# A bidirectional Mamba-2 mixer on one core: square sums between the halves of the output projection, D x ahead of x times the step sizes, and decays and step sizes at other places

## The chip, the cores and the metric

The kernel runs on one core of one Trainium2 chip. A core has a matrix engine (TensorE, PE in the profile; PEld is the loading of its weights), a vector engine (VectorE, DVE), an activation engine (ScalarE, ACT), a general engine (GpSimd, POOL), and an engine that here only starts transfers (SyncE, SP). Each engine has its own queue and takes its instructions in that order; between engines they wait for one another's results. SBUF is the memory on the chip, PSUM the one that TensorE writes to.

The metric is the time of one launch on the device in microseconds. Before the change its median is 1506.12 us over three runs (1503.04 to 1506.87). The profiled execution spans 1499.7 us. All data are fp32.

## What is computed

The input is an image batch of 8 x 32 x 32 x 128, that is 8 sequences of 1024 tokens with 128 channels. Three residual parts follow one another: attention, the mixer, and a spectral filter. Only the mixer concerns us. For each sequence it runs twice, forward (`d = 0`) and backward in time (`d = 1`), with two sets of weights, and adds both to the residual:

```python
def _mamba3(x, in_proj, conv_w, conv_b, A_log, dt_bias, D, norm_w, out_proj):   # x: layer-normed tokens
    z, xbc, dt = split(x @ in_proj)
    xbc = silu(conv(xbc, 4 taps) + conv_b)
    xh, Bm, Cm = split(xbc)                       # 4 heads of 64; state of 64
    dt = softplus(dt + dt_bias);  A = -exp(A_log)
    y = _ssd(xh, dt, A, Bm, Cm) + xh * D          # "D x"
    yg = y * silu(z)
    yn = yg * rsqrt(mean(yg * yg, -1) + EPS) * norm_w     # "square sums"
    return yn @ out_proj

def _ssd(xh, dt, A, Bm, Cm):                      # chunks of 64 tokens
    xdt = xh * dt[..., None];  dA = dt * A        # "x times step sizes", decays
    Acs = cumsum(dA within a chunk)
    Y_diag = (C B^T * exp(segment sums of dA)) @ xdt
    states = B^T @ (exp(Acs_last - Acs) * xdt)    # one for each chunk
    prev   = scan over chunks: state = states + state * exp(Acs_last)
    Y_off  = exp(Acs) * C @ prev
    return Y_diag + Y_off

h = _mamba3(x, fwd...) + _mamba3(x[:, ::-1], bwd...)[:, ::-1]
t = t + h
```

## The kernel before

The mixer works through 16 units, one for each sequence and direction: (b, 0), (b, 1), for b from 0 to 7. In a unit, x and its gates lie channel by token as two tiles of 128 x 1024 (`n = 0, 1`); what goes into the states lies token by channel. The units are interleaved by hand three deep: one pass of the loop at L1169 does the middle of unit `u`, the beginning of unit `following`, and the end of unit `last`. The loop stands under a manual schedule in which each engine takes its instructions in the order in which the program issues them. So the order of the calls in the loop is the order of each queue, and a call that stands earlier is not only earlier itself: what stands behind it on the same engine waits with it.

In the order of one pass, with the lines that later steps name:

- `turn_decays` and `take_decays` of `following` (L807, L813): the cumulated decays, turned by TensorE, their exponentials on ScalarE, and a trip through memory (`cd`) that brings them back as rows for all partitions in `lm` and `ec`. `between(u, Exp)` (L852, L855) is ScalarE's exponential over `lm`, two pieces of 128 x 1024.
- `turn_x` (L940): 16 transposes of x into two PSUM buffers (`sx`, L948), each followed by VectorE's multiplication with the step sizes, `xdt` (L951). `weigh_start` (L859) multiplies `ec` with C on GpSimd. `add_x(last)` (L1068) is D x of the unit before, added to its outputs in PSUM (`y`, L1074).
- `turn_b` (L958): B and C B^T into one PSUM buffer (`sb`), copied by ScalarE (`bg`, L973). In a forward unit, `turn_tokens` then turns the next sequence's tokens (`px`, copied to `xt`).
- `project_x(following, n)` (L877): `pp`, its copy to `xp` on ScalarE (L886); `first_tap` (L889, L891) begins the convolution over 4 tokens on ScalarE. `gate(last, n)` (L1083): VectorE's product with silu(z) (L1085) and ScalarE's square (L1086). `decayed_x`: `xdd` (L982).
- In a forward unit, the first part of `steps` (L476) for the next sequence: `pd` (L491) on TensorE, `sp_v` (L499), L501 and L502 on VectorE, an exponential on ScalarE (L503), L505 on VectorE. The parts behind its two `yield`s, the logarithm (L508) and L510 to L515, come after `add_up`.
- `project_out(last)` (L1088): `spo`, 16 calls that the trace counts as 32 matmuls (L1092). `square_sums` (L1100): eight matmuls with a matrix of ones into `misc` (L1104), copied by ScalarE to `sums` (L1112). `turn_sums` (L1114): two transposes back into `misc` (L1118), `rms_v` on VectorE (L1120) and the power -1/2 on GpSimd, `rms` (L1122). `add_up` (L1126, L1129): the residual takes `spo` times `rms`.
- The three taps of the convolution on VectorE (`convolve`, L895, L899): those of half 0 lie between the square sums and the add-up, those of half 1 near the end of the pass. `project_z` (L906): `pz` and its silu (L910). `activate_x` (L903, L904): silu of the convolved x.
- `normalize` and `normalized` (L442, L451): in a backward unit, the layer norm of the sequence after the next: `bn_stats`, a power on GpSimd, the shift (L453), and eight pieces of `ln_x` on ScalarE (L458).
- `from_row` (L842, L846): GpSimd forms `lm` = cs - row for `following`. It is made to wait for the last tap that was issued ("beside the states"), so that it runs beside the state steps.
- `chunk_states` (L986): `pst`, two PSUM buffers. `pass_states` (L1003): 28 short steps on VectorE (L1012). `weigh_decays` (L1030, L1034), `between(following, Relu)`, `project_bc` and `activate_bc` (L912 to L935) of `following`: `pb` on TensorE and four silus.
- `outputs(u, 0)` and `outputs(u, 1)` (L1038): `sy`, the matmuls at L1060, with `add_decays` (L792: `pdec` on TensorE, two copies on ScalarE) of the unit after the next between them.

PSUM is the scarce memory: `ps_w` and `ps_s` are two pools of two buffers each, every buffer 128 x 1024. `sx`, `sb`, `px`, `pp`, `pd`, `pz`, `pb` and `pdec` take turns in `ps_w`; `spo`, `misc`, `pst` and `sy` in `ps_s`. A buffer is written again only when its last reader is done.

Of the kernel before, what the change touches and what calls it, by code (L numbers as in the profile page):

```python
# [9 lines left out]
AF = mybir.ActivationFunctionType  # L10
# [4 lines left out]
P = 128  # L15
B = 8
T = 1024
NT = T // P
# [27 lines left out]
def fast_kernel(ctx: ExitStack, tc: tile.TileContext, a: dict, out: bass.AP, bad: bass.AP):  # L46
# [713 lines left out]
    with ExitStack() as s:  # L760
# [104 lines left out]
        def projected(u, cols, name):  # L865
            ps = wide_psum(ps_w, name)
            for i in range(2):
                nc.tensor.matmul(
                    ps[:, i * 512 : (i + 1) * 512],
                    lhsT=win[u.d][:, cols],  # L870
                    rhs=u.seq["xt"][:, pad + i * 512 : pad + (i + 1) * 512],
                    start=True,
                    stop=True,
                )
            return ps

        def project_x(u, n):  # L877

            if n == 0:
                u.xs = p2.tile([P, 2, T], F32, tag="xs", name=f"xs{u.tag}")  # L880
                u.xp = []
            pp = projected(u, slice(DI + n * P, DI + (n + 1) * P), f"pp{u.tag}_{n}")
            xp = p2.tile([P, T + pad], F32, tag="xp", name=f"xp{u.tag}_{n}")
            body, edge = (slice(pad, T + pad), slice(0, pad)) if u.d == 0 else (slice(0, T), slice(T, T + pad))
            nc.gpsimd.memset(xp[:, edge], 0.0)
            nc.scalar.copy(xp[:, body], pp)  # L886
            u.xp.append((xp, body))
# [18 lines left out]
        def project_z(u, n):  # L906
            if n == 0:
                u.zs = p2.tile([P, 2, T], F32, tag="zs", name=f"zs{u.tag}")
            pz = projected(u, slice(n * P, (n + 1) * P), f"pz{u.tag}_{n}")
            nc.scalar.activation(u.zs[:, n, :], pz, AF.Silu)  # L910

# [175 lines left out]

        def project_out(u):  # L1088
            u.po = wide_psum(ps_s, f"spo{u.tag}").rearrange("p (j e) -> p j e", j=NT)
            for j in range(NT):  # L1090
                for n in range(2):
                    nc.tensor.matmul(  # L1092
                        u.po[:, j, :],
                        lhsT=u.y[:, n, j * P : (j + 1) * P],
                        rhs=wo[u.d][:, n, :],
                        start=(n == 0),
                        stop=(n == 1),
                    )
# [48 lines left out]
        s.enter_context(tc.manual_schedule(engines=ALL_IN_ORDER))  # L1147
        first, norms, av = units[0], {}, avs[1]
        add_decays(first)
        turn_decays(first)  # L1150
# [3 lines left out]
        for n in range(2):  # L1154
            project_x(first, n)
            first_tap(first, n)
        convolve(first, 0)
# [7 lines left out]
        compare_denominators(most, least, wide_psum(ps_w, "pf")[0:1, :2])  # L1165
        add_decays(units[1])

        last = None
        for at, u in enumerate(units):  # L1169
            following = units[at + 1] if at + 1 < len(units) else None  # L1170

            fresh = u.b + 1 if u.d == 0 and u.b + 1 < B else 0
            if following:
                turn_decays(following)
            if at == 0:
                between(u, AF.Relu, 1.0)
            if following:
                take_decays(following)
            between(u, AF.Exp, -1.0)
            turn_x(u)  # L1180
            weigh_start(u, u.convolved)
            if last:
                add_x(last)
            turn_b(u)
            if fresh:
                turn_tokens(fresh, seqs[fresh], wide_psum(ps_w, f"px{fresh}"))
            if following:
                project_x(following, 0)
                first_tap(following, 0)
            if last:  # L1190
# [3 lines left out]
            if last:  # L1194
                gate(last, 1)
            decayed_x(u)
            going = iter(())
            if fresh:
                going = steps(fresh, seqs[fresh], wide_psum(ps_w, f"pd{fresh}"))
                next(going)  # L1200
                next(going)
            if last:
                project_out(last)
                misc = wide_psum(ps_s, f"misc{last.tag}")
                square_sums(last, misc)
            if following:
                first_tap(following, 1)
                convolve(following, 0, range(pad - 1))
            if last:
                turn_sums(last, misc)  # L1210
            if following:
                convolve(following, 0, range(pad - 1, pad))
            project_z(u, 0)
            project_z(u, 1)
            if following:
                activate_x(following, 0)
# [8 lines left out]
            pass_states(u)  # L1225
            if norm:
                for _ in normalized(b, bridge, *norm):
                    pass
            if last and last.d == 1:
# [8 lines left out]
            outputs(u, 0)  # L1238
            if at + 2 < len(units):
                add_decays(units[at + 2])  # L1240
            if following:
                activate_x(following, 1)
            outputs(u, 1)
            last = u
        add_x(last)
        for n in range(2):
            gate(last, n)
        project_out(last)
        misc = wide_psum(ps_s, f"misc{last.tag}")
        square_sums(last, misc)  # L1250
        turn_sums(last, misc)
        add_up(last)
# [1068 lines left out]
```

## Time and profile before

| Stage (us of the span) | PE | DVE | ACT | POOL | clock |
|---|---|---|---|---|---|
| attention, 0 to 456 | 431.62 | 360.53 | 293.52 | 235.17 | 0.98 |
| mixer, 456 to 1086 | 544.79 | 495.30 | 397.16 | 186.31 | 0.96 |
| transform, 1086 to 1176 | 85.09 | 45.05 | 43.11 | 61.30 | 0.97 |
| frequencies, 1176 to 1450 | 266.33 | 201.16 | 149.56 | 32.96 | 0.99 |
| inverse, output, 1450 to 1500 | 30.98 | 21.17 | 0.00 | 0.00 | 0.84 |

The columns are busy microseconds of each engine in the stage, from the table by windows; the last is the mean clock that TensorE was granted, as a share of full speed. A stage of 630 us in which TensorE is busy for 545 and VectorE for 495 has a good deal of idle time on every engine. In the page's list of groups the costliest of the mixer are these (mean duration of one, and how many):

| Group | mean ns | count |
|---|---|---|
| L859 `ec` on POOL, 128x2048 | 4532 | 16 |
| L899 tap on DVE, 128x1024 | 1282 | 96 |
| L919 `pb` on PE, 128x512 | 598 | 256 |
| L1012 state step on DVE, 128x64 | 275 | 448 |
| L951 `xdt` on DVE, 128x1024 | 1221 | 32 |
| L1122 `rms` on POOL, 128x8 | 2455 | 16 |

A line of an engine's order of time gives the start in the span, the time to the end of the group, the engine, the line, the operation, out<-in with shape, the count, and in brackets how long the engine was idle before it and whose result ended that.

### The profile page before, as it was taken

Reading aid. Unit: us, or ns where it says so; the run is one execution under the profiler, and the core shown is the slowest. Engines: PE = TensorE matmul, PEld = TensorE weight load, DVE = VectorE, ACT = ScalarE, POOL = GpSimd, SP = SyncE. Lnnn points to the kernel's source line nnn. Section 1 sums busy time; section 2 is a strip of 40 time slices with the busy share of each in tenths; the row PEclk is TensorE's granted clock in tenths of the full one; section 3 lists DMA queues with packets and bytes.
Section 4 is the critical chain, followed back from the end, with each engine's and each line's share of the span. In section 5 each row is a group of like instructions: output and inputs, shape, how many; then the busy total and the mean of one; then the engine's idle time right before and its main releaser. Section 6 shows DMA issues by size and latency. Waiting matters only on the chain.

```text
span 1499.7 us, 45232 instructions
## 1 busy us (share of the span) xinstructions
PE 1358.8 (91%) x19782; PEld 855.7 (57%) x19782; DVE 1123.2 (75%) x2250; ACT 883.4 (59%) x1293; POOL 515.7 (34%) x510
## 2 busy tenths in 40 slices
PE   5999999999998989888988898897589899999977
PEld 2333323333334656565655666665479898999962
DVE  5788888788766788888888787886655577777744
ACT  2766666676676666666676667664155455555520
POOL 2336866776202232323232323233177211111100
PEclk9999999999999899999999999999799999999989
DMA  7001111110003333343334343341158522232258
GB/s 184 28 1 29 54 33 43 50 43 8 1 1 82 79 82 93 80 98 79 97 80 93 78 100 78 86 86 43 37 175 218 148 74 67 73 86 74 67 144 313
DMA packets 139382, 123.09 MB, mean 82 GB/s; under 512 B 44808, under 2 KB 118152, under 8 KB 135080
## 3 DMA queue, kind: packets, MB, share of 16 engines
q1 hardware_dynamic: 137064, 115.93, 30.2%
q10 hardware_dynamic: 2112, 4.19, 0.7%
q8 instruction: 157, 2.57, 0.7%
q14 instruction: 49, 0.40, 0.1%
HBM read 78.15 MB, written 34.08 MB: 75 GB/s over the span
## 4 chain that ended last, share of the span: by engine, by line
PE 57%; DVE 17%; issue 11%; ACT 7%; POOL 6%; DMA 2%; DVEq 0%; ACTq 0%; SPq 0%; POOLq 0%
PE pg L1382 9%; PE pt L626 9%; PE py L1416 8%; PE po L647 7%; DVE state L1012 5%; PE pd L667 4%; PE sy L1060 3%; POOL rms L1122 3%; PE spo L1092 2%; DVE X L1129 2%; ACT ln_x L458 2%; PE pf L1300 2%; POOL ec L859 2%; DVE xdt L951 1%; DVE y L1074 1%
## 5 line engine op out<-in xcount | busy, mean ns | idle before, releaser
L631 ACT ACTIVATE pr<-pt 128x1024 f32<-128x1024 f32 x256 | 248.1, 1021 | 115.2 <-PE pt L626 113.5
L656 DVE TENSOR_TENSOR two<-pr,pr 128x1024 f32<-128x1024 f32 x128 | 163.1, 1315 | 20.4 <-ACT pr L631 19.5
L1393 DVE COPY gs<-pg 128x512 f32<-128x512 f32 x256 | 158.7, 684 | 17.8 <-PE pg L1382 12.8
L1395 ACT COPY gs<-pg 128x512 f32<-128x512 f32 x256 | 132.6, 603 | 66.9 <-PE pg L1382 51.0
L626 PE MATMUL pt<-q,k 32*128 32x512 f32 x1024 | 159.8, 654 | 7.0 <-ACT pr L631 4.5
L1382 PE MATMUL pg<-taps,mst 32*128 32x128 f32 x4096 | 146.9, 281 | 6.0 <-ACT gs L1395 3.4
L1382 PEld LDWEIGHTS pg<-taps,mst 32*128 32x128 f32 x4096 | 133.7, 188 | 19.3 <-issue 14.0
L647 PE MATMUL po<-pr,v 128*32 128x512 f32 x1024 | 140.2, 606 | 0.0
L859 POOL TENSOR_TENSOR ec<-ec,ct 128x2048 f32<-128x2048 f32 x16 | 72.5, 4532 | 164.8 <-issue 90.6
L1416 PE MATMUL py<-gs,u 128*32 128x128 f32 (+1 forms) x4096 | 127.8, 277 | 0.0
L899 DVE SCALAR_TENSOR_TENSOR xs<-xp,cw,xs 128x1024 f32<-128x1024 f32 x96 | 123.0, 1282 | 4.3 <-issue 2.6
L1416 PEld LDWEIGHTS py<-gs,u 128*32 128x32 f32 (+1 forms) x4096 | 112.0, 141 | 7.2
L919 PE MATMUL pb<-bxt,wbc 128*128 128x512 f32 x256 | 114.2, 598 | 0.2 <-ACT xp L886 0.2
L1122 POOL TENSOR_TENSOR rms<-rms_v,mhalf 128x8 f32<-128x8 f32 x16 | 39.3, 2455 | 213.8 <-DVE rms_v L1120 213.8
L1405 POOL TENSOR_SCALAR u<-u 128x512 f32<-128x512 f32 x16 | 24.0, 1497 | 229.0 <-DMA u<-ud 113.5
L626 PEld LDWEIGHTS pt<-q,k 32*128 32x128 f32 x1024 | 47.6, 187 | 84.9 <-issue 33.0
L1012 DVE SCALAR_TENSOR_TENSOR state<-state,dec,pst 128x64 f32<-128x64 f32 x448 | 87.3, 275 | 1.2
L458 ACT ACTIVATE ln_x<-X,b_shift,ln_r 128x128 f32<-128x128 f32 x128 | 51.2, 482 | 60.8 <-DVE b_shift L453 60.8
L951 DVE TENSOR_TENSOR xdt<-sx,dt 128x1024 f32<-128x1024 f32 x32 | 38.1, 1221 | 60.4 <-PE sx L948 60.4
L1060 PE MATMUL sy<-lm,xdt 64*64 64x64 f32 x2048 | 69.4, 229 | 14.7 <-DVE lm L1034 11.5
L919 PEld LDWEIGHTS pb<-bxt,wbc 128*128 128x128 f32 x256 | 47.1, 189 | 56.8 <-issue 56.4
L1060 PEld LDWEIGHTS sy<-lm,xdt 64*64 64x64 f32 x2048 | 63.0, 140 | 28.0 <-issue 27.3
(277 smaller groups left out, 2789.2 us busy)
## 6 DMA issues: line engine op xcount, KB each, us to landing
lm<-cd SPq DMA_DIRECT2D x32, 512.0 KB
ec<-cd SPq DMA_DIRECT2D x32, 512.0 KB
ud<-sp SPq DMA_DIRECT2D x8, 1024.0 KB
u<-ud SPq DMA_DIRECT2D x32, 256.0 KB
yd<-sums SPq DMA_DIRECT2D x32, 256.0 KB
moved<-state SPq DMA_DIRECT2D x48, 128.0 KB
yt<-yd SPq DMA_DIRECT2D x6, 1024.0 KB
X<-in_x SPq DMA_DIRECT2D x8, 512.0 KB
```

What stands on the lines that cost most here:

```text
L626: nc.tensor.matmul(pt[:, i, :], lhsT=k[rows, j * P : (j + 1) * P], rhs=q[rows, cols], start=True, stop=True)
L631: nc.scalar.activation(pr[:, 2 * g : 2 * g + 2, :].rearrange("p i t -> p (i t)"), pt.rearrange("p i t -> p (i t)"), AF.Exp, scale=SCALE,)
L647: nc.tensor.matmul(po[rows, :], lhsT=vs[b][:, j, rows], rhs=pr[:, h, :], start=(j == 0), stop=(j == NT - 1))
L656: nc.vector.tensor_tensor(two, sums["pr"][:, 2 * g : 2 * g + 2, :], pr[:, 2 * g : 2 * g + 2, :], ALU.add)
L899: u.convolved = nc.vector.scalar_tensor_tensor(acc, xp[:, at : at + T], cw[u.d][:, n, i : i + 1], acc, ALU.mult, ALU.add)
L919: nc.tensor.matmul(u.pb[:, i * 512 : (i + 1) * 512], lhsT=wbc[u.d][:, k, :], rhs=xt[:, at : at + 512], start=(k == 0), stop=(k == KC - 1),)
L1012: nc.vector.scalar_tensor_tensor(u.state[:, k, h, :], u.state[:, k - 1, h, :], u.dec[:, c, h, j : j + 1], u.pst[c][:, j, h, :], ALU.mult, ...
L1060: nc.tensor.matmul(u.py[c][h * HP : (h + 1) * HP, r, j, :], lhsT=left, rhs=right, start=(kind == 0), stop=(kind == 1 or k is None),)
L1382: nc.tensor.matmul(pts[g][:, e, :], lhsT=mst[rows, n * 4 + e, :], rhs=taps[rows, cols].rearrange("p f q m i -> p (f q m i)"), start=True, ...
L1393: nc.vector.tensor_copy(to, frm)
L1395: nc.scalar.copy(to, frm)
L1416: nc.tensor.matmul(py[t * 32 : t * 32 + 32 - 16 * m, q // 2, :], lhsT=u[:, i, m:, :, :, q * FC + f].rearrange("p k b i -> p (k b i)"), rhs ...
```

## The change

The calls of one pass are put in another order, and three functions are split in two so that their parts can be placed apart. No computation is added or left out. There are five parts:

1. **D x first.** `add_x(last)` moves ahead of `turn_x(u)`, so that VectorE can add D x while TensorE still turns x.
2. **Square sums between the halves of the output projection.** `project_out` does four of the eight token blocks at a time, and the new `end` puts `square_sums` between the halves, so that the sums' copy on ScalarE can run beside the second half. `project_x` is split from its copy, `copy_x`; the second copy now stands behind the squares on ScalarE.
3. **Decays at other places.** In a backward pass the decays of the unit after the next (`after_it`) are added behind `turn_sums` and turned behind the first `project_z`, instead of between the outputs and at the next pass's start; in a forward pass `add_decays` stays between the outputs and `turn_decays` at the start of the next. `activate_z` is split off so that the pieces fit between. The exponential over `lm` moves from the start of the pass to a place behind these.
4. **Step sizes later.** The first part of `steps` moves from ahead of the output projection to behind the last tap, right ahead of `project_z` and `add_up`.
5. **The layer norm in halves.** `normalized` does four of its eight pieces where it did all, and the other four ahead of `outputs(u, 1)`.

The diff, without the declarations of the split functions `copy_x` and `activate_z`:

```diff
+        def end(u):
+            project_out(u, 0)
+            u.misc = wide_psum(ps_s, f"misc{u.tag}")
+            square_sums(u, u.misc)
+            project_out(u, 1)
...
+        add_decays(units[1])
+        turn_decays(units[1])
         convolve(first, 0)
...
-        add_decays(units[1])
...
-            if following:
+            if following and u.d == 1:
                 turn_decays(following)
             if at == 0:
                 between(u, AF.Relu, 1.0)
             if following:
                 take_decays(following)
-            between(u, AF.Exp, -1.0)
+            if last:
+                add_x(last)
             turn_x(u)
             weigh_start(u, u.convolved)
-            if last:
-                add_x(last)
             turn_b(u)
...
             if following:
                 project_x(following, 1)
             if last:
                 gate(last, 1)
+            if following:
+                copy_x(following, 1)
             decayed_x(u)
+            if last:
+                end(last)
+            if following:
+                first_tap(following, 1)
+                convolve(following, 0, range(pad - 1))
+            if last:
+                turn_sums(last, last.misc)
+            early_decays = after_it and u.d == 1
+            if early_decays:
+                add_decays(after_it)
+            else:
+                between(u, AF.Exp, -1.0)
+            if following:
+                convolve(following, 0, range(pad - 1, pad))
             going = iter(())
             if fresh:
                 going = steps(fresh, seqs[fresh], wide_psum(ps_w, f"pd{fresh}"))
                 next(going)
                 next(going)
-            if last:
-                project_out(last)
-                misc = wide_psum(ps_s, f"misc{last.tag}")
-                square_sums(last, misc)
-            if following:
-                first_tap(following, 1)
-                convolve(following, 0, range(pad - 1))
-            if last:
-                turn_sums(last, misc)
-            if following:
-                convolve(following, 0, range(pad - 1, pad))
             project_z(u, 0)
+            if early_decays:
+                turn_decays(after_it)
+                between(u, AF.Exp, -1.0)
+            activate_z(u, 0)
             project_z(u, 1)
+            activate_z(u, 1)
...
-            if norm:
-                for _ in normalized(b, bridge, *norm):
-                    pass
+            norming = normalized(b, bridge, *norm) if norm else iter(())
+            next(norming, None)
...
             outputs(u, 0)
-            if at + 2 < len(units):
-                add_decays(units[at + 2])
+            if after_it and not early_decays:
+                add_decays(after_it)
             if following:
                 activate_x(following, 1)
+            next(norming, None)
             outputs(u, 1)
```

## The prediction

> **What bounds the kernel now.** I read the page first, then the busy table by window, then the instructions in order of time of one steady pair of units (about 701 to 813 us). The change touches only the mixer, some 470 to 1086 us. The window table, cut at each unit's first xdt (L951), says that no engine is full there:
>
> ```profile
> 701.43:738.96 37.53, 33.99 (x509) 23.46 (x508) 30.78 (x66) 24.81 (x34) 10.86 (x8) 1.00 0.41 100
> 738.96:775.24 36.28, 31.99 (x485) 21.16 (x484) 30.06 (x74) 25.29 (x38) 12.57 (x8) 1.00 0.33 74
> ```
>
> Columns: stretch, length, then busy us of PE, PEld, DVE, ACT, POOL, then the clock. A forward unit (d=0, first line) takes 37.5 us and a backward one (d=1, second line) 36.3, with VectorE busy 30 of them. So a unit is a chain through four in-order queues, and what counts is which wait ends last. A backward unit in order of time (VectorE, then TensorE, then ScalarE):
>
> ```profile
> 738.96 2.36 DVE L951 TENSOR_TENSOR xdt<-sx,dt 128x1024 f32<-128x1024 f32 x2 [2.71 <-PE sx L948]
> 741.23 2.71 DVE L1074 SCALAR_TENSOR_TENSOR y<-xs,dcol,sy 128x512 f32<-128x512 f32 x4
> 743.86 2.35 DVE L1085 TENSOR_TENSOR y<-y,zs 128x1024 f32<-128x1024 f32 x2
> 751.92 0.17 DVE L1120 TENSOR_SCALAR rms_v<-misc 128x8 f32<-128x8 f32 x1 [0.32 <-PE misc L1118]
> 754.81 2.16 DVE L1129 SCALAR_TENSOR_TENSOR X<-spo,rms,X 128x128 f32<-128x128 f32 x8 [1.53 <-POOL rms L1122]
> ```
> ```profile
> 745.79 4.09 PE L1092 MATMUL spo<-wo,y 128*128 128x128 f32 x32
> 749.81 1.07 PE L1104 MATMUL misc<-zs,ones 128*32 128x256 f32 x16
> 751.38 0.44 PE L1118 MATMUL misc<-ident,sums 128*128 128x128 f32 x2 [0.49 <-ACT sums L1112]
> ```
> ```profile
> 764.93 3.19 ACT L458 ACTIVATE ln_x<-X,b_shift,ln_r 128x128 f32<-128x128 f32 x8 [7.67 <-DVE b_shift L453]
> 768.03 1.99 ACT L855 ACTIVATE lm<-lm 128x1024 f32<-128x1024 f32 x2
> 773.11 1.06 ACT L904 ACTIVATE xs<-xs 128x1024 f32<-128x1024 f32 x1
> ```
>
> Call S the end of the last output matmul (sy, L1060): 737.73, then 773.2. VectorE stands idle until the turned x exists, then does xdt, D x (y, L1074) and the gates one after another. rms_v (call it R) comes at S+14.2, after projection, square sums, their copy and two transposes. GpSimd's pow holds VectorE until the add-up (L1129), which frees the PSUM buffer for the states. The end is ScalarE's: it idles 7.67 us for the layer norm's shift, then runs 3.19 of normalizing, 2.0 of lm, the B and C activations and the copies of the decays; only then comes the second silu (773.11), which the next turn waits for (1.0 us after S). In the forward unit R is at S+17.6 (790.82), and TensorE sets the end: the states wait for the add-up, pb follows, outputs and pdec run to about S+38.3.
>
> **What the Trainium skill says.** "SBUF — State Buffer", section "Who interferes with whom": a VectorE instruction with two SBUF inputs, or in a two-port mode, and a GpSimd instruction that reads SBUF exclude each other, and the later one waits. The trace agrees for a long GpSimd operation:
>
> ```profile
> 793.64 3.62 POOL L846 TENSOR_TENSOR lm<-cs,lm 128x2048 f32<-128x2048 f32 x1
> 795.78 1.56 DVE L510 SCALAR_TENSOR_TENSOR sp_u<-sp_u,sp_e 128x64 f32<-128x64 f32 x1
> ```
>
> L510 takes 0.22 us in the first unit, where nothing is in its way, and 1.56 here, ending as lm ends. For a pow the trace differs from "the whole instruction": around 173 us a pow waited for one `two` (L656), yet the next `two` beside it kept its 1.2 us. I take it that a pow excludes others at its ends only. "TensorE: Matmul & The Clock Gate", section "What's actually happening": after an idle window TensorE falls to half clock for at least 3.4 us. The trace agrees: most units show clock 1.00, three forward ones 0.96 to 0.97, the thin last unit 0.83. "ScalarE: Activation LUTs", section "What ACT_TABLE_LOAD costs": 1283 ns a load; here 1.28, and both kernels have the same number of them.
>
> **The change part by part** (no arithmetic is added or removed; times from S).
>
> *D x first.* VectorE begins y (2.63) at S and no longer waits for the transposes; xdt follows at S+2.7 and gates end at S+7.2, against 9.2 (forward) and 8.4 (backward). But B and C (sb) take sx's PSUM buffer, which the first xdt frees: xdt to sb is 1.28 in the trace, so sb starts at S+4.0, against 2.5 (backward) and 3.3 (forward), and all of TensorE's projections move with it.
>
> *Square sums between halves.* Backward: sb 4.0 to 6.0, two pp (1.77 each) to 9.5, half of spo (1.9) to 11.4. The squares, now ahead of the second x copy, end at S+12.15 (sb +2.13 bg, pp +2.02 copy, +1.04, +1.15, two squares of 1.0). Sums end at 12.7, second half at 14.6, during which ScalarE copies the sums; R = 14.6+0.55 = S+15.15. That is 0.95 later than before: 1.5 lost at sb, 0.5 won at the sums copy. Forward: px adds 1.2, sb 4.0, pp 7.15 to 10.7, half 12.6, sums 13.95, rest 15.85, R = S+16.4, against 17.6: pd (1.7) has gone behind R, which pays for the later sb.
>
> *Normalizing in two halves, decays early.* Backward: add-up R+2.88 to R+5.05 = 20.2, bn 2.15, states 5.7, shift at S+28.15, four ln_x to 29.9 instead of eight, lm 31.9, B and C 34.65, silu to 35.7 without the two decay copies: the turn starts at S+35.8, before 36.5. TensorE: z waits for early decays, their turn, exp and table load: z0 at S+22.75, so pb 22.8 to 29.85 (before 28.3), but pdec (1.3 and up to 0.6 of gap) is gone from between the outputs: S' = S+34.9 against 35.5. The other four ln_x lie beside TensorE's turn and cost nothing.
>
> *Step sizes behind the last tap (forward).* Ahead of the add-up VectorE now has sp_v, L501, L502, a trip to ScalarE, and L505; behind them in its queue are add-up and states, for which TensorE's states wait. pd starts at R-0.28; pd to sp_v is 1.89 in the first unit and sp_v to L505 1.03, so L505 is at R+2.65 to R+2.85. pow ends at R+2.85 and lm starts there. So L505 just passes, and the add-up starts at R+2.9, as now. The three earlier ones run inside pow's middle. Bound from the other side: L505 meets lm and waits 3.6. The L510 stall stays. Exp of lm on ScalarE ends at about R+1.3, ahead of its part. Add-up ends S+21.45, states 23.4, pb 30.5, outputs, pdec and outputs 6.5 to 6.7: S' = S+37.1, against 38.3.
>
> Sum of a pair: 34.9+37.1 = 72.0; before 37.53+36.28 = 73.8. Won: 1.8 to 1.9, six times = 11.4. First unit: the waiting turn of decays (2.0 idle before 477) goes, but last_py and pb come later and lm meets L501: 1.5 won. Forward unit 7, without step sizes: 1.2. Last unit and its tail: D x first 1.3, sums copy 0.9: 2.2. In all 16.3. Against it: TensorE now idles about 2 us between sx and sb in a backward unit (before 0.4), and may fall to half clock; at 1.7 us a time I book two more such windows, 3 us. 1506.1-16.3+3 = **1493 us**.
>
> **Rivals.**
> A, *lm wins the race.* L505, 0 to 0.2 us ahead in my sum, loses. The add-up moves from R+2.9 to R+6.7; TensorE idles 3.5 us more, the forward unit ends 3.7 later (the L510 stall goes, but TensorE sets the end), the pair is 1.85 slower than before, six times 11, and half clock after such an idle stretch about 6 more; 5 won elsewhere stay: 1518. For it: L511 (two SBUF inputs) in the first unit waited 3.67 behind lm. Against: the measured steps leave it just ahead. If only half of the units lose, 1505.
> B, *the clock takes it.* The later sb makes a half-clock window in half of the 15 units (1.7 each, 12 in all, not 3): 1502, with the 0.5 us gaps that nothing explains up to 1508. For it: forward units already lose clock at this place. Against: 1.4 us of idle before the states (757.02) never cost clock.
> C, *ScalarE was the bound*: with both silus 1 us earlier in every unit and no loss at sb, 1486.
>
> **How the numbers follow.** Mine 0.56, A 0.20, B 0.16, C 0.08. Faster than 1501.6: mine, C and a part of B, 0.71; within 0.3%: most of B and the mixed form of A, 0.11; slower: A, 0.18. Range 1484 to 1511: C at one end, half of A's way at the other.
>
> **What would show it.** In the new profile: y (D x) starts at the end of sy and xdt has no wait for sx; sb waits longer for xdt; R at about S+15 and S+16.4; no wait for the sums copy; ln_x in two groups of four; L505 (0.20) ahead of add-up, which waits only for pow; L510 still about 1.5. Wrong if L501, L502 or L505 takes over 1 us and the add-up follows lm's end; if units with clock under 0.97 are more than five; or if backward units do not end on ScalarE's silu.

## The result, and the profile after

The changed kernel takes 1491.5 us, median of four runs (1489.06 to 1493.92), beside 1506.03 before; the ratio is 0.9907, 95% interval 0.9885 to 0.9929. The profiled execution spans 1489.0 us, 10.7 less than the 1499.7 of before; the medians differ by 14.5, so the tables below, which come from the two profiles, account for the 10.7.

The same table by windows as before, for a forward and the backward unit after it, cut at the first xdt (now L955). Columns: stretch, length, busy us of PE, PEld, DVE, ACT, POOL, then the clock, DMA share and GB/s:

```profile
843.60:880.02 36.42, 33.97 (x507) 23.37 (x507) 30.93 (x66) 26.03 (x38) 10.94 (x8) 1.00 0.43 103
880.02:915.30 35.28, 31.34 (x483) 20.40 (x483) 30.18 (x75) 23.66 (x33) 12.63 (x8) 1.00 0.36 76
```

71.7 us for the pair, beside 73.8 in the pair that was shown of before, with nearly the same busy time on VectorE (61.1 and 60.8). Both are quick pairs: over six pairs the mean is 72.6, and it was 74.7. The backward unit in order of time on VectorE; its outputs' last matmul (S) ends at 877.25:

```profile
877.38 2.72 DVE L1078 SCALAR_TENSOR_TENSOR y<-xs,dcol,sy 128x512 f32<-128x512 f32 x4 [0.86 <-PE sy L1064]
880.02 2.35 DVE L955 TENSOR_TENSOR xdt<-sx,dt 128x1024 f32<-128x1024 f32 x2
882.28 2.35 DVE L1089 TENSOR_TENSOR y<-y,zs 128x1024 f32<-128x1024 f32 x2
892.51 0.17 DVE L1125 TENSOR_SCALAR rms_v<-misc 128x8 f32<-128x8 f32 x1 [2.19 <-PE misc L1123]
895.40 2.16 DVE L1134 SCALAR_TENSOR_TENSOR X<-spo,rms,X 128x128 f32<-128x128 f32 x8 [1.53 <-POOL rms L1127]
```

D x (y) begins 0.13 us after S and xdt has no wait in brackets: the turn of x lies beside D x. rms_v, R, stands at S+15.26, where it was S+14.3 before. (That is the instant that the prediction calls S+14.2; S is read as 737.58 here for its 737.73.) TensorE of the same unit:

```profile
881.29 1.15 PE L969 MATMUL sb<-ident,bt 64*64 64x64 f32 x32 [1.77 <-DVE xdt L955]
886.85 1.95 PE L1097 MATMUL spo<-wo,y 128*128 128x128 f32 x16
889.56 0.64 PE L1109 MATMUL misc<-zs,ones 128*32 128x256 f32 x8 [0.20 <-ACT zs L1090]
890.13 2.05 PE L1097 MATMUL spo<-wo,y 128*128 128x128 f32 x16
892.02 0.38 PE L1123 MATMUL misc<-ident,sums 128*128 128x128 f32 x2
```

The transposes of the sums (L1123) follow the second half without a wait; before, they waited 0.49 us for the copy of the sums. The price stands in the first line: sb waits 1.77 us for xdt (S+4.04), and the projection starts 2.2 us after the gates have ended (884.63). The forward unit around its R (857.27):

```profile
857.52 2.64 POOL L1127 TENSOR_TENSOR rms<-rms_v,mhalf 128x8 f32<-128x8 f32 x1 [12.44 <-DVE rms_v L1125]
860.09 3.62 POOL L846 TENSOR_TENSOR lm<-cs,lm 128x2048 f32<-128x2048 f32 x1
```
```profile
859.92 0.20 DVE L505 TENSOR_SCALAR sp_u<-sp_e 128x64 f32<-128x64 f32 x1 [0.32 <-ACT sp_e L503]
860.20 2.16 DVE L1134 SCALAR_TENSOR_TENSOR X<-spo,rms,X 128x128 f32<-128x128 f32 x8
862.27 1.52 DVE L510 SCALAR_TENSOR_TENSOR sp_u<-sp_u,sp_e 128x64 f32<-128x64 f32 x1
```

L505 starts 0.17 us ahead of GpSimd's lm (0.52 in one of the six passes, 0.17 in the others) and takes its 0.20; L510, behind the add-up, takes 1.52, until lm ends.

Where the time went, from the ends of the outputs in the two profiles (us):

| Stretch | before | after | difference |
|---|---|---|---|
| first pdec to the end of the first unit's outputs | 57.29 | 57.08 | -0.2 |
| the next unit | 34.03 | 35.21 | +1.2 |
| six pairs | 447.95 | 435.56 | -12.4 |
| the two units after them | 69.52 | 67.44 | -2.1 |
| the rest, to the end | 433.47 | 435.35 | +1.9 |

The attention ahead of the first pdec took 457.40 and 458.38; neither it nor the code from the last unit's end on was changed, apart from that unit's tail. The six pairs are the gain, 2.07 us each.

Within a pair the cut matters. From S to S, the backward passes grew from 34.2 to 35.4 us on average, and the forward ones shrank from 40.4 to 37.2. The same pair before and after, first its backward and then its forward pass:

```profile
663.77:697.82 34.05, 31.50 (x492) 21.06 (x483) 30.06 (x74) 22.78 (x33) 11.01 (x7) 1.00 0.36 79
697.82:737.58 39.76, 34.27 (x514) 23.48 (x507) 30.78 (x65) 27.33 (x38) 11.97 (x8) 1.00 0.39 94
```
```profile
660.17:695.50 35.33, 31.29 (x494) 20.50 (x485) 30.17 (x74) 23.17 (x34) 11.58 (x8) 1.00 0.35 77
695.50:732.53 37.03, 33.87 (x515) 23.15 (x507) 30.93 (x65) 26.39 (x37) 11.39 (x8) 1.00 0.43 101
```

Before, TensorE was done with the outputs of the backward unit at 697.82 and then waited, for ScalarE's copy of the decays and for its second silu, which ended 2.54 us later:

```profile
699.05 0.22 ACT L804 COPY dsum<-pdec 128x96 f32<-128x96 f32 x1
699.30 1.06 ACT L904 ACTIVATE xs<-xs 128x1024 f32<-128x1024 f32 x1
```

In five of the six forward passes of before it stood so (end of the silu at S+2.5 to 2.8); in the changed kernel that silu ends 0.3 to 0.9 us after S, and D x lies beside what is left of the wait. The pass that the prediction read, behind 773.2, is the sixth, with 1.0.

### The profile page after: what moved, and what is told of

It is laid out like the page before. It is cut to its first block, busy times and chain, and to the rows that moved or that the text cites. A ratio compares the mean times of both kernels' runs of the same rounds, so it can differ in the third digit from the quotient of the medians.

```text
span 1489.0 us, 45246 instructions
## 1 busy us (share of the span) xinstructions
PE 1351.5 (91%) x19782; PEld 843.7 (57%) x19782; DVE 1124.6 (76%) x2250; ACT 878.9 (59%) x1293; POOL 516.0 (35%) x510
## 4 chain that ended last, share of the span: by engine, by line
PE 60%; DVE 14%; issue 10%; ACT 9%; POOL 4%; DMA 2%; DVEq 0%; SPq 0%; ACTq 0%; POOLq 0%
PE pg L1407 10%; PE pt L626 9%; PE py L1441 8%; PE po L647 7%; DVE state L1016 4%; PE pd L667 4%; PE sy L1064 3%; PE pb L923 2%; POOL ec L859 2%; PE pf L1325 2%; PE pz L868 2%; ACT ln_x L458 2%; POOL rms L1127 1%; DVE y L1078 1%; PE pz L1520 1%
## 5 line engine op out<-in xcount | busy, mean ns | idle before, releaser
L656 DVE TENSOR_TENSOR two<-pr,pr 128x1024 f32<-128x1024 f32 x128 | 162.8, 1312 | 19.4 <-ACT pr L631 18.5
L901 DVE SCALAR_TENSOR_TENSOR xs<-xp,cw,xs 128x1024 f32<-128x1024 f32 x96 | 123.1, 1283 | 16.3 <-ACT xs L893 12.8
L923 PE MATMUL pb<-bxt,wbc 128*128 128x512 f32 x256 | 117.3, 612 | 7.2 <-ACT zs L914 7.2
L1064 PE MATMUL sy<-lm,xdt 64*64 64x64 f32 x2048 | 67.5, 227 | 16.8 <-DVE lm L1038 9.5
L647 PEld LDWEIGHTS po<-pr,v 128*32 128x32 f32 x1024 | 28.1, 110 | 88.4 <-issue 84.5
L458 ACT ACTIVATE ln_x<-X,b_shift,ln_r 128x128 f32<-128x128 f32 x128 | 51.8, 481 | 37.2 <-DVE b_shift L453 37.2
```

The lines of the kernel that those rows point to most:

```text
L647: nc.tensor.matmul(po[rows, :], lhsT=vs[b][:, j, rows], rhs=pr[:, h, :], start=(j == 0), stop=(j == NT - 1))
L656: nc.vector.tensor_tensor(two, sums["pr"][:, 2 * g : 2 * g + 2, :], pr[:, 2 * g : 2 * g + 2, :], ALU.add)
L901: u.convolved = nc.vector.scalar_tensor_tensor(acc, xp[:, at : at + T], cw[u.d][:, n, i : i + 1], acc, ALU.mult, ALU.add)
L923: nc.tensor.matmul(u.pb[:, i * 512 : (i + 1) * 512], lhsT=wbc[u.d][:, k, :], rhs=xt[:, at : at + 512], start=(k == 0), stop=(k == KC - 1),)
L1064: nc.tensor.matmul(u.py[c][h * HP : (h + 1) * HP, r, j, :], lhsT=left, rhs=right, start=(kind == 0), stop=(kind == 1 or k is None),)
```

## The experiments

R is rms_v, S the end of the last output matmul of the unit before it, as in the prediction. All differences named without a partner are against the changed kernel's 1491.5.

### D x back behind x times step sizes

```diff
-            if last:
-                add_x(last)
             turn_x(u)
             weigh_start(u, u.convolved)
+            if last:
+                add_x(last)
```

> The changed kernel, but with D x back behind x times step sizes, as before. Theory (the working of the prediction): D x first lets B and C start 1.3 us later in every unit, because they take the PSUM buffer that xdt frees, and the gates that it brings forward by 1.2 us are not waited for (in the changed kernel they end at S+7.4, the half projection starts at about S+9.6). So undoing it must gain: sb at S+2.65 instead of 4.05 in a backward pass, about S+2.9 in a forward one (the turn waits for the silu there), rms_v about 1.4 and 1.1 us earlier, a pair of units 72.2 - 2.5 = 69.7, in all some 15 us less than the changed kernel: 1474 to 1480. Rival: D x first is what pays, through gates and squares; then rms_v stays or moves later, and the time goes back by 5 to 15 us, to 1497 to 1506.

Measured: 1477.93 us (1473.17 to 1481.98), ratio to before 0.9821 (0.9785 to 0.9857), 13.6 less than the changed kernel. TensorE of a backward unit, S at 864.63:

```profile
867.29 1.15 PE L969 MATMUL sb<-ident,bt 64*64 64x64 f32 x32 [0.44 <-DVE xdt L955]
872.85 2.30 PE L1097 MATMUL spo<-wo,y 128*128 128x128 f32 x16
875.08 1.12 PE L1109 MATMUL misc<-zs,ones 128*32 128x256 f32 x16
```

sb starts at S+2.66 instead of 4.04, and everything behind it moves with it: R at S+13.95, and S+15.64 in the forward unit before, where the changed kernel has 15.26 and 16.45. The gates end later (S+8.6), but the projection starts at S+8.2, just ahead of the second gate's end, no longer 2.2 us behind it. Six pairs take 419.9 us instead of 435.6. So D x first is a loss within this change, and the other parts gain more than the whole.

### D x first alone, on the kernel before

```diff
+            if last:
+                add_x(last)
             turn_x(u)
             weigh_start(u, u.convolved)
-            if last:
-                add_x(last)
```

> The kernel before with D x ahead of x times step sizes as its only change. Theory: in a forward pass the turned x waits for ScalarE's late silu anyway (xdt at S+3.6), so y fills that time, but what follows (sb, pp, pd, the projection) is TensorE's and not the gates': R stays at S+19.2 to 20. In a backward pass sb moves from S+2.65 to 4.05 and R by up to 1.4 later. So it makes the kernel before slower: 7 passes of 1.0 to 1.4, 7 to 10 us, 1513. Rival: y in the shadow of the turn gains 1 to 2 us in each forward pass, 8 or more less, 1497.

Measured: 1511.96 us (1505.89 to 1518.35), ratio to before 1.0054 (1.0021 to 1.0087): slower, by 7 us. R moves from S+14.34 to about S+15.4 in backward passes; in forward ones it stays within what it was (17.6 to 20.5 before, 18.3 to 20.5 here), because xdt waits for ScalarE's late silu either way. The loss needs no other part of the change.

### Square sums behind both halves

```diff
             project_out(u, 0)
+            project_out(u, 1)
             u.misc = wide_psum(ps_s, f"misc{u.tag}")
             square_sums(u, u.misc)
-            project_out(u, 1)
```

> The changed kernel, but with the square sums behind both halves of the output projection. Theory: the sums' copy and its way to the transposes lie open again, 0.4 us in each unit (rms_v 2.23 us after the end of the projection as in the kernel before, instead of 0.5 us after a second half that ends 1.7 later): rms_v at S+15.65 and S+16.85, 15 units of 0.4, the time 5 to 6 us longer than the changed kernel: 1497. Rival: the place of the sums is the main part of the gain, then 10 or more longer.

Measured: 1496.06 us (1490.66 to 1500.76), ratio to before 0.9945 (0.9921 to 0.9968), 4.6 longer, near the 5 to 6 expected, but not for the reason; the two intervals (the changed kernel's ends at 0.9929) still touch. R is only 0.11 later in both kinds of pass (S+15.37 and 16.56), as the 0.49 us for the copy is nearly paid by the squares, which the sums then no longer wait for (0.20 us). In two of the six forward passes of the profile z's projection takes 5.38 instead of 3.69 us, and these passes show clocks of 0.95 and 0.96; these two are 3.4 us. The part is worth about 1.7 us by R; the rest is open.

### One more instruction ahead of L505

```diff
         e = small("sp_e")
         nc.vector.tensor_scalar(e, v, -1.0, None, ALU.mult)
+        nc.vector.tensor_scalar(e, v, -1.0, None, ALU.mult)
```

> The changed kernel with the small instruction L501 done twice (0.2 us more ahead of L505; same result). Theory: L505 ends at R+2.85 in the changed kernel just as GpSimd's lm starts (0.02 us between them); 0.22 us later it meets lm and waits 3.6 us, with the add-up and TensorE's states behind it: forward units 3 to 3.6 longer in six passes, 18 to 22 us longer than the changed kernel, 1510 to 1513, and L505 at 3.6 to 3.8 us where it was 0.2. Rival: the two do not exclude each other at this place, then 0.2 us in each of seven passes, 1.5 us longer, 1493.

Measured: 1517.99 us (1517.33 to 1524.47), ratio to before 1.0103 (1.0069 to 1.0137), 26.5 longer. A forward unit, GpSimd and then VectorE (L505 is L506 here):

```profile
875.02 3.61 POOL L847 TENSOR_TENSOR lm<-cs,lm 128x2048 f32<-128x2048 f32 x1
```
```profile
875.08 3.60 DVE L506 TENSOR_SCALAR sp_u<-sp_e 128x64 f32<-128x64 f32 x1 [0.32 <-ACT sp_e L504]
878.61 2.15 DVE L1135 SCALAR_TENSOR_TENSOR X<-spo,rms,X 128x128 f32<-128x128 f32 x8
880.67 0.21 DVE L511 SCALAR_TENSOR_TENSOR sp_u<-sp_u,sp_e 128x64 f32<-128x64 f32 x1
```

An instruction of 0.2 us that starts 0.06 us after lm lasts until lm ends, the add-up stands behind it at S+22.85 instead of 19.4, and the states with it. The forward passes of the six pairs take 40.2 to 42.1 us, where they took 36.4 to 38.6. Six times 3.5 are 21; the rest goes with five passes of the six pairs at clocks of 0.95 and 0.96, where the changed kernel has two at 0.95 and 0.98 and one at 0.97. This is the prediction's rival A, brought about by one small instruction: 1518 was its time, and it had booked 6 us for the clock. The changed kernel stays clear of it by 0.17 us.

### lm behind the step sizes

```diff
-        nc.vector.tensor_tensor(
+        seq["stepped"] = nc.vector.tensor_tensor(
             da.rearrange("p d h j -> p j d h"),
...
-                from_row(following, following.convolved)
+                from_row(following, seqs[fresh]["stepped"] if fresh else following.convolved)
```

> The changed kernel, but in a forward pass GpSimd's lm is made to wait for the last instruction of the step sizes (L515) instead of the last tap. Theory: L510 takes 0.22 instead of 1.5 us, so the states start 1.3 us earlier; weighing then ends ahead of pb, and TensorE's pb sets the start of the outputs: 0.9 us less in each of six forward passes; the first pass loses its 3.6 us wait of L501 and part of TensorE's 4.2 us wait before pb: 3.5. In all 9 us less than the changed kernel, 1482 (L501 0.2 everywhere). Rival: lm, 3 us later, makes its Relu late and ScalarE's end with it: no gain, 1491 or more.

Measured: 1487.71 us (1486.16 to 1488.3), ratio to before 0.9884 (0.9858 to 0.9909), 3.8 less, not 9. The first pass is what was expected of it and more. In the changed kernel GpSimd's lm, VectorE's L501, ScalarE's silu of z, which stands behind the exponential of the step sizes (L503), and TensorE's pb of that pass read:

```profile
493.42 3.62 POOL L846 TENSOR_TENSOR lm<-cs,lm 128x2048 f32<-128x2048 f32 x1 [8.88 <-DVE xs L901]
```
```profile
493.51 3.58 DVE L501 TENSOR_SCALAR sp_e<-sp_v 128x64 f32<-128x64 f32 x1
```
```profile
497.39 0.26 ACT L503 ACTIVATE sp_e<-sp_e 128x64 f32<-128x64 f32 x1 [4.01 <-DVE sp_e L502]
500.52 1.94 ACT L914 ACTIVATE zs<-pz 128x1024 f32<-128x1024 f32 x2
```
```profile
501.60 8.83 PE L923 MATMUL pb<-bxt,wbc 128*128 128x512 f32 x16 [4.17 <-ACT zs L914]
```

and with lm behind the step sizes:

```profile
493.54 0.19 DVE L501 TENSOR_SCALAR sp_e<-sp_v 128x64 f32<-128x64 f32 x1
```
```profile
498.24 7.14 PE L923 MATMUL pb<-bxt,wbc 128*128 128x512 f32 x16 [0.79 <-ACT zs L914]
```

52.01 us to the end of the first unit's outputs instead of 57.08: 3.4 of wait, and 1.7 because pb no longer runs slower after it. The two intervals overlap, so it is this pass and not the medians that shows the gain; the six pairs of the profile are 3.0 longer (438.6 us), with one backward pass of 36.6 at a clock of 0.95 and two passes of 37.4 and 38.8 with more and longer pauses in the outputs (see the decays below). In the six forward passes L510 takes 0.22 us, as expected, but the states start only 0.2 earlier (S+23.5, before 23.7):

```profile
860.27 2.05 PE L999 MATMUL pst<-xdd,bg 64*64 64x128 f32 x64
```
```profile
860.22 0.22 DVE L510 SCALAR_TENSOR_TENSOR sp_u<-sp_u,sp_e 128x64 f32<-128x64 f32 x1
860.99 0.28 DVE L515 TENSOR_TENSOR da<-dt,nega 128x64 f32<-128x64 f32 x1
862.28 0.29 DVE L1013 COPY state<-pst 128x128 f32<-128x128 f32 x1 [1.02 <-PE pst L999]
```

The first copy of the states waits for pst's 2.05 us of matmuls, which start only when the add-up has freed their PSUM buffer. L510's stall lies beside them and costs 0.2 us, not 1.3.

### Step sizes ahead of the output projection

```diff
             decayed_x(u)
+            going = iter(())
+            if fresh:
+                going = steps(fresh, seqs[fresh], wide_psum(ps_w, f"pd{fresh}"))
+                next(going)
+                next(going)
             if last:
                 end(last)
...
-            going = iter(())
-            if fresh:
-                going = steps(fresh, seqs[fresh], wide_psum(ps_w, f"pd{fresh}"))
-                next(going)
-                next(going)
             project_z(u, 0)
```

> The changed kernel, but with the first part of the step sizes (pd, sp_v, L501, L502, L505 and the two logarithm steps on ScalarE) back ahead of the output projection. Theory: TensorE's pd, 1.7 us, stands ahead of R (rms_v) again in six forward passes: R at S+18.1 instead of 16.45, and the end 1.7 us later each, 10 us; the first pass wins back about 4 (no L501 behind lm, no late silu of z). Sum: 6 us longer than the changed kernel, 1497. Rival: pd was hidden anyway, then only the first pass counts: 1487.

Measured: 1500.91 us (1495.26 to 1510.6), ratio to before 0.9975 (0.996 to 0.999), 9.4 longer. TensorE of a forward unit, S at 844.13:

```profile
854.92 1.85 PE L491 MATMUL pd<-wdt,bxt 128*128 128x8 f32 x16
856.62 2.03 PE L1097 MATMUL spo<-wo,y 128*128 128x128 f32 x16
```

R is at S+17.82 instead of 16.45, 1.4 of pd's 1.7 (0.2 of the difference is the wait for the squares, which is gone). The profiled execution shows 446.5 us for the six pairs, 11 longer than the changed kernel, and 2.1 less in the first pass. Half of the 11 is one forward pass of 42.2 us at a clock of 0.92; the other five are 1.1 longer each, near what R is later. ScalarE also changes its function table seven times more here (53 table loads in the program, 46 in the changed kernel), but from R to the end of a pass nothing is later than in the changed kernel. So pd stood on the path, and moving it behind R is one of the gains.

### The layer norm in one piece

```diff
             norming = normalized(b, bridge, *norm) if norm else iter(())
-            next(norming, None)
+            for _ in norming:
+                pass
...
-            next(norming, None)
             outputs(u, 1)
```

> The changed kernel, but with all eight pieces of ln_x in one place, ahead of lm's Relu. Theory: in six backward passes ScalarE's second silu ends 1.65 us later (S+37.4 instead of 35.7), TensorE's end S' stays at S+35.2; D x first hides most of it, because y fills 2.65 us while x is turned, so only about 0.6 us of each forward pass is lost (sb at S+4.65 instead of 4.05): 3 to 4 us longer than the changed kernel, 1495. Rival (the prediction's own words, a backward unit ends on ScalarE): 1.65 in each of six, 10 us, 1501.

Measured: 1499.64 us (1491.65 to 1504.07), ratio to before 0.9965 (0.995 to 0.998), 8.1 longer, between theory and rival. The silu of backward passes ends at S+37.3 as expected. sb of the forward pass behind it starts at S+4.57 to 5.64 in five of six passes (the sixth: 4.08), and in four of them it also runs slower:

```profile
548.59 2.43 PE L952 MATMUL sx<-ident,xs 128*128 128x128 f32 x15 [1.92 <-ACT xs L906]
550.95 1.98 PE L969 MATMUL sb<-ident,bt 64*64 64x64 f32 x32
552.71 1.29 PE L969 MATMUL sb<-ct,bt 64*64 64x64 f32 x32
```

The turn waits 1.92 us for the silu, and sb's first half takes 1.98 where it takes 1.15. The units that show it have clocks of 0.92 to 0.96. Over the six forward passes sb starts 4.5 us later and R comes 8.3 later than in the changed kernel: in this profile the halves of the layer norm gain about as much by sparing TensorE a slow window as by the wait itself. Two backward passes ran slow as well (36.6 and 37.3 us, clock 0.95), behind sb's wait for xdt, which the changed kernel has too; these are not the layer norm's.

### Decays late in backward passes

```diff
-            if following and u.d == 1:
+            if following and at > 0:
                 turn_decays(following)
...
-            early_decays = after_it and u.d == 1
+            early_decays = False
```

> The changed kernel, but with the decays of backward passes back between the outputs and their turn at the next pass's start (those of the second unit stay early). Theory: pdec lies between the outputs again, 1.3 us and up to 0.6 of gap on TensorE, less the 0.4 us that z's silu and pb then start earlier: S' at S+36.5 instead of 35.2 in seven backward passes, 9 us longer than the changed kernel, 1500. Rival: ScalarE's silu (S+35.7) is the end of a backward pass and covers it: 2 to 4 us.

Measured: 1490.17 us (1486.65 to 1498.72), ratio to before 0.991 (0.9881 to 0.9939): no difference from the changed kernel. Backward passes take 34.1 to 35.0 us and one 37.1, in the changed kernel 34.6 to 35.3 and one 37.0. The waits of TensorE in the outputs of one backward unit, in the changed kernel (us in total, times, longest):

```profile
PE sy L1064 <- issue: 1.3, 1, 1.3
```

With late decays the same view of the same unit is empty, and pdec stands there instead, from 909.42 to 910.6. "issue" is a wait for nothing that the profile shows. It comes once in most units, mostly 0.5 to 1.6 us, at a place in the stream that moves by 4 or 26 matmuls from unit to unit (after 151, 155, 181, 185, 211, 215 and 241 of the 248 in the second to the eighth unit of the changed kernel), so it belongs to no operation. The changed kernel has it in all seven backward passes, 0.8 to 1.4 us; where pdec stands between the outputs, in the kernel before and with late decays, only one of the seven has it. The 1.2 us that the early decays take off TensorE there return as this gap.

The trace's DMA packets give a hint at what it waits for. Each of the changed kernel's 13 pauses ends 1.2 to 1.6 us after the end of a packet of 16 KB on the queue that the profile calls "instruction"; so do the seven of the kernel before and the seven with late decays. In the backward passes where pdec divides the outputs and no pause is seen, such a packet ends while pdec runs or within 0.2 us of its end. So the pause looks like TensorE waiting for its next instructions. No run changes when they come, so this is not tested.

### Combinations

The first takes D x back and puts lm behind the step sizes; the second moves all of ln_x behind the second silu as well:

```diff
             norming = normalized(b, bridge, *norm) if norm else iter(())
-            next(norming, None)
...
-            next(norming, None)
+            for _ in norming:
+                pass
             outputs(u, 1)
```

The third is the first with late decays.

> The changed kernel with D x back behind x times step sizes and, in forward passes, GpSimd's lm behind the step sizes. Theory: the two gains lie at different places (sb and the first pass) and add: 13.6 + 3.8 less than the changed kernel, 1474. Rival: the first pass's gain is lost again to windows of half clock: 1478 as with D x alone.

> As dx_after_lm_behind, and all eight pieces of ln_x behind ScalarE's second silu. Theory: without D x in its shadow the turn of forward passes waits for that silu (xdt at S+1.2 to 2.0 where S+1.37 is what the turn takes); the silu ends 1.65 us earlier, all forward passes have xdt at S+1.4, 0.3 us on average in six passes: 2 us less than dx_after_lm_behind, 1472. Rival: ln_x then delays the exponentials of the decays and B and C's copy in the next pass: sb to pp later, 3 us or more longer.

> As dx_after_lm_behind, with the decays of backward passes late as in decays_late. Theory from decays_late (no difference): the gap without a releaser in the outputs, 0.9 to 1.5 us, is absent where pdec stands between the outputs of a backward pass, and takes pdec's place where it does not; so again no difference, 1474, S' of backward passes within 0.5 of dx_after_lm_behind. Rival: pdec lies open, 1.3 us in seven passes, 9 us longer.

Measured: 1471.87 us (1468.39 to 1475.36), ratio to before 0.9792 (0.9752 to 0.9832); 1471.51 (1470.86 to 1474.31), 0.9781 (0.9746 to 0.9815); 1478.73 (1475.82 to 1483.98), 0.9835 (0.9793 to 0.9877). In the first the gains add, as the profile has it: 52.00 us to the first outputs' end and 419.05 for the six pairs, beside 52.01 with lm behind alone and 419.9 with D x back alone; by the medians its interval overlaps that of D x back alone. A clean pair of it, from the table by windows, takes 68.88 us:

```profile
826.30:861.17 34.87, 33.96 (x509) 23.36 (x508) 29.60 (x65) 26.09 (x36) 10.80 (x8) 1.00 0.46 108
861.17:895.18 34.01, 31.37 (x485) 20.50 (x484) 30.05 (x75) 23.59 (x37) 12.75 (x8) 1.00 0.38 79
```

ln_x last changes nothing: sb of forward passes stands at S+2.48 in three of six, the full gain of the theory, but R of the six is at S+15.7 on average and not 15.3, so theory and rival both hold in part and cancel. Late decays cost 6.9 here (the intervals overlap a little), though not on their own: with their turn at the pass's start, x's turn waits 0.63 us between its halves for ScalarE's copy of the decays (cs, L811), and D x follows the start of xdt by 2.86 us instead of 2.28; with D x ahead of xdt that was hidden, here it moves R of forward passes to S+15.8 to 16.3. That is some 0.5 in six passes; part of the rest goes with clocks of 0.93 to 0.98 in four units, and what makes them slow there is not shown. So the first combination, 1471.9, is the shortest with the least change: 20 us less than the changed kernel, 33 less than before.

## Why the prediction was right, and where not

It gave 1493 and faster; measured was 1491.5. The order of the steps and most of their times came as forecast, but the total is nearer than its parts, and in that there is luck. By its steps:

- **D x first**: right in its times (sb at S+4.0, measured 4.04; R at 15.15 and 16.4, measured 15.26 and 16.45). It booked the later sb as a debit inside a gain of 1.8 a pair, and never asked what the pair would be without it. The runs with and without say 13.6 us.
- **Square sums between halves**: the wait for the copy is gone as said. The 0.5 us of the term is 0.11 when the part alone is undone, as the sums otherwise wait for the squares.
- **Step sizes behind the last tap**: right, and its narrowest step. L505 at R+2.65, lm at R+2.82 (forecast 2.65 to 2.85 and 2.85); 0.2 us more turned it into rival A, at A's time. pd's 1.7 came back as 1.4 in R when put ahead.
- **Layer norm in halves**: the silu at S+35.7 is as forecast (35.7), and R and sb show no cost of the four other pieces. The silu is hardly the end of the unit any more, though: S' is at 34.6 to 35.3 in five of six passes, and D x covers the rest.
- **Decays early**: the step failed. "pdec is gone from between the outputs" is true, but the outputs of a backward pass take 5.1 to 5.6 us, and in six of the seven passes of before they took 5.4 to 5.7; a pause of about pdec's length took its place. The price of pdec and its gap was read from the seventh, the pass up to 773.2, in which the outputs took 7.1 us with two waits of 0.58 and 0.71 for nothing that the profile shows. Its S' of 35.5 was 33.8 to 34.05 in the other five of the six pairs. So S', forecast as 34.9 and 0.6 earlier, came at about 35.0, which is 1.0 later. pb was summed to 29.85 and ended at 29.97.
- **What the pair read did not show**: in five of six forward passes of before the silu came at S+2.5 to 2.8, and TensorE waited for it and for ScalarE's copy of the decays. The prediction's times from S are read in the sixth, where it came at 1.0, so it could not count how much an earlier silu gives back in the others (R, 17.6 there, is at 19.2 to 20.5 in them, and at 16.4 to 16.8 in the changed kernel). The 38.3 for the end of a forward pass stands in no pass either: the one read ends at S+39.2, and 38.3 is what 35.5 leaves of 73.8. So the forward passes won 3.2 us and not 1.2, while the backward ones lost 1.1.
- **L510**: its 1.5 us stays, as said, but costs only 0.2.
- **The first unit**: the largest miss. 1.5 us won was the term; 0.2 was measured. (The 1.2 us that the next unit is longer is what all backward passes show when cut at S.) lm meeting L501 was foreseen, but not that z's silu stands behind the same step sizes on ScalarE, that pb waits for it 4.17 us, and that it then runs slower. lm_behind_steps shows 5.1 us there.
- **Rival C** (1486) took away the loss at sb, which the likeliest case kept. With D x back that loss is gone, and the time is 1478.
- **The clock**: 3 us were booked for two more slow windows. Between the first unit and the last, the profile before has three stretches of 3.4 us at a granted clock of 0.5, in the late turn of x of forward passes, and the profile after has two: one lies where the prediction put it, behind a wait of 1.88 us for xdt (pp, below, takes 4.88 instead of 3.71 us, and R comes 1.6 later), the other in the outputs of a later pass. So on balance nothing was lost, and rival B did not come. D x alone on the kernel before has five such stretches beside three, and the changed kernel with D x back has one beside two: the direction is the one foreseen, the size small, and each is one profile.

```profile
739.07 4.88 PE L868 MATMUL pp<-bxt,win 128*128 128x512 f32 x8
```

The sums: six pairs 12.4 (forecast 11.4); the first two units lost 1.0 (forecast 1.5 won); the last two won 2.1, and R of the last one 0.5 (forecast together 3.4). In these stretches 14.0 was won, and 16.3 was forecast; the 3 us booked for the clock stood against the miss in the first unit, so that the 1493 came out near. The 1.9 us of the rest and the 1.0 of the attention lie in unchanged code, apart from the 0.5.

The parts undone one at a time come to 9.4 for the step sizes, 8.1 for the layer norm, 4.6 for the square sums, nothing for the decays and 13.6 against for D x. They sum to 8.5 and not to 14.5; they act on one another. One such link is seen: D x hides a part of the late silu of an undivided layer norm (sb 0.8 later for a silu 1.65 later, in the pass in which TensorE keeps its speed). The others were not taken apart, and the new places of the second copy of x and of lm's exponential were not undone by themselves.

## What to carry to other kernels

When a part of a change is forecast to lose in one place and win in another, price the change without it, too; the prediction's own sums had both numbers (the gates end at S+7.2, the projection starts at S+9.5), and their difference, 2.3 us of slack, was the answer. Read several passes before one is taken as the steady one: the pair that was priced here was the one pass in seven with a pause at pdec, and the one in six with a short wait for the silu. Ask of each stall what stands beside it: L510's 1.5 us cost 0.2, while 3.6 us on a first unit's L501 cost 5.1 through a silu and a buffer two engines away. A small instruction that just passes a long one on another engine is a margin to measure, and here one dependency moved (lm behind the step sizes) removes it.

## What the runs showed of the hardware

- A one-input 128x64 VectorE instruction of 0.2 us lasts 3.60 us when it starts 0.06 us after GpSimd's 128x2048 subtraction, and 0.20 when it starts 0.17 us ahead of it.
- Inside GpSimd's power of 128x8 (857.52 to 860.16 in the changed kernel) three VectorE instructions of 128x64, L501, L502 and L505, kept their 0.20, 0.23 and 0.20 us.
- TensorE's outputs, 248 short matmuls of 64x64, pause once in most units, mostly for 0.5 to 1.6 us, with no releaser in the profile, at a place that shifts with the stream; in six of seven backward passes not where pdec, 1.2 us of small matmuls, divides them. Each pause of the three profiles that were looked at ends 1.2 to 1.6 us after a 16 KB packet on the DMA queue of instructions.
- After a wait of 1.9 us for the silu, sb's first half took 1.8 to 1.98 instead of 1.15 us in four passes; after one of 2.12 us, in a fifth, it took 1.15. After a wait of 4.17, pb took 8.83 instead of 7.14. A wait of 1.0 to 2.0 for xdt, which every pass of the changed kernel has, was followed by such a slow stretch in one pass of the 15.
